# A graph layer on one core: one edge tile in 24 fetched row by row, and a reordered end

## The chip, the cores and the metric

The kernel runs on one core of a Trainium2 chip. Its time is the device time of one execution in microseconds (us). Several runs of the kernel before and after are compared, and one execution of each is profiled: every instruction of every engine with start and duration, and every DMA packet. The engines are PE (matmuls), DVE (vector), ACT (scalar), POOL (GpSimd) and SP (which only issues DMAs). SP and ACT each have a queue that issues plain DMAs in order. POOL issues indirect DMAs (gathers), whose descriptors it writes itself.

## What is computed

A relational graph convolution behind a layer norm, on 12500 nodes of 256 features and 212500 edges of 8 types; the edges are sorted by destination, and each node's last edge is its self loop:

```
h = maximum(layernorm(x), 0)
hx = einsum('ni,rio->rno', h, weight)        # 8 types
msg = hx[edge_type, src]
agg = segment_sum(msg, dst, 12500)
out = x + agg * sqrt(0.5) + bias + (h @ loop_weight) * sqrt(0.5)
```

The kernel sums the rows of h by destination and type first and multiplies by the weights afterwards, which gives the same.

## The kernel before

**Edge tiles.** Edges go in 1581 tiles of 128; two tiles are a unit (791 units, the last with one tile). For each tile the rows `h[src]` of its 128 edges come into a buffer `msg` of 128 x 256 (1 KB a row). DVE makes one-hot columns by (destination, type) (line 992, four tiles at a time), PE multiplies the rows with them (`edge_sums`, line 1030, four matmul instructions a tile), and DVE adds a unit's sums into a ring `acc` of node columns (`add_sums`, line 1063). A tile's one-hots reach over 13 of 22 destination columns (104 wide) or 17 (136 wide: `REACH`), but for the units of the last block from row `NARROWED` on, which take the whole width (176); `TAPER` sets how many units that is at the end.

**Where the rows come from.** The first tiles are gathered from x and normalised in place; in the meantime the kernel normalises x into a table h32 in HBM, and from then on tiles are gathered from that. Line 935 is the gather: one indirect DMA on POOL for a tile. `goal(t)` says how far gathers are emitted ahead of tile t: 64 tiles at first, falling to 24 at tile 370, and to 8 at the end. A ring of 66 buffers (33 pairs) holds the tiles.

**Tiles fetched row by row.** A tile with `t % SINGLE == SINGLE - 1` (SINGLE = 28), once h32 has been in use for a while and 16 tiles before the end at the latest (`single_rows`, line 907), isn't gathered. `begin_fetch` takes its buffer FAR = 36 tiles ahead, or when its gather would be emitted if that is earlier; HOLD = 8 tiles later SP and ACT each load 2 x 32 row addresses into registers (line 956) and issue 64 plain DMAs of 1 KB (line 964), four queue items on each per tile of the loop (`fetch`). PE waits by count for all 128 rows (line 1027).

**Node groups.** Nodes go in 98 groups, the first of 84 nodes and the others of 128; the ring holds six (SLOTS). When a group's last unit is added, `group_work` puts its work into `queue`: 2 products of its own rows with the loop weight and 16 with the types' weights (line 1237, two matmul instructions each), then `finish`: two additions on DVE (lines 1225 and 1252), and the store to `out`. Groups go in sets of four (XG). A set's rows of x and h come with one load each on SP (line 1180), into one of 6 row buffers in turn; the result replaces the x rows, and is stored from there. `finish` stores a whole set with one DMA of 512 KB (line 1257) at its last group, and single groups (128 KB, line 1254) for the first group and for the last set (groups 96 and 97). It then also clears or begins a ring slot, and starts loads of later sets. Every sixth group `wrap` adds the ring's overlap to its start (line 1209).

**The order of the work** is the order of emission in the loop over tiles, written out by hand: fetches and gathers, one-hots, edge sums of tile t, `finish` of groups that are due, side work, items from `queue`, and then the sums of finished units (`add_sums`), which put groups into the queue. The queue is spread: each item has a tile from which it may be issued (`ready`) and one by which it must (`until`), and a budget per tile is worked out from these. Each engine runs its instructions in this order. In the last SOON = 8 units sums are added without a lag of one unit; for the last 8 groups `ready` is the next tile and `until` at most six tiles after it.

Of the kernel before, what the change touches and what calls it, by code (L numbers as in the profile page):

```python
# [20 lines left out]
SP = mybir.EngineType.SP  # L21
ACT = mybir.EngineType.Activation

P = 128
# [4 lines left out]
XG = 4  # L29
# [13 lines left out]


WIN = 22
TAPER = 4
REACH = ((0, 13), (5, 17))

GROUP = 128
# [11 lines left out]
NEXT = 24  # L61
CLOSE = 8

SINGLE = 28
FETCH = 4
SOURCES = 32
BY_SP = (0, 2)
HOLD = 8
FAR = 36
COUNTERS = 4  # L70
LANDINGS = 68

# [3 lines left out]
PAIR = 2  # L76
# [6 lines left out]
SOON = 8  # L83
# [165 lines left out]
def kernel(  # L249
# [11 lines left out]
    nc = tc.nc  # L261
# [8 lines left out]
    plan = Plan(N, E)  # L270

    NT = plan.NT
# [41 lines left out]

    NARROWED = max(0, (row_of(NU - 1)[1] + 1 - TAPER) // PAIR * PAIR)

# [11 lines left out]
    with ExitStack() as main:  # L328
# [29 lines left out]
        msg, oh, offsets, kind = {}, {}, {}, {}  # L358
        firsts, stops, loops, marked, typed, gidx, col = {}, {}, {}, {}, {}, {}, {}
        added, zeroed = {}, {}  # L360
        single, fetches = {}, {SP: [], ACT: []}
        counters = [tc.alloc_semaphore(f"rows{i}") for i in range(COUNTERS)]
        fetched, summed = {}, {}
        landings = [tc.alloc_semaphore(f"landed{i}") for i in range(LANDINGS)]
# [389 lines left out]
        done = {"norm": 0, "weights": False, "late": [], "tile": None, "free": 0, "step": False}  # L754
# [50 lines left out]
        for d in range(0, N, XG * P):  # L805
            k = min(XG, (N - d) // P)
# [98 lines left out]
        def single_rows(t):  # L905

            return (t % SINGLE == SINGLE - 1 and t + 2 * NEAR < NT
                    and state["h32"] is not None and t // QUAD * QUAD >= state["h32"] + LATE + AHEAD)
# [67 lines left out]
        def fetch(n):  # L976
            for list_ in fetches.values():
                for _ in range(n):
                    if list_ and list_[0][0] <= done["tile"]:
                        list_.pop(0)[1]()  # L980
# [184 lines left out]
        def shorts(q):  # L1165

            return int(plan.ends[XG * q] - plan.starts[XG * q] < P)
# [46 lines left out]
        def group_work(g):  # L1214

            d0 = plan.starts[g]
            s0, n = slot(g)
            first_dep = [True]
            final = plan.NG - 1 if plan.NG > SLOTS + 1 else None

            def biased(g):
                q, k = divmod(g, XG)
                n = plan.ends[g] - plan.starts[g]
                rows_ = got["x", q]
                nc.vector.tensor_add(rows_[:n, k, :], rows_[:n, k, :], outs[g % 2][:n, 1, :])  # L1225

            def product(r, c, g=g):
                n = plan.ends[g] - plan.starts[g]
                if (r, c) == (R, 0):
                    got["out", g] = outs[g % 2][:, 0, :]  # L1230
                if r == R:
                    while ("self", g) not in got:
                        advance(None)
                    lhs, rhs = got["self", g][:, c, :n], wl[:, c, :]
                else:
                    lhs, rhs = acc[:, c, r, s0 : s0 + n], w[:, c, r * D : (r + 1) * D]
                i = nc.tensor.matmul(got["out", g][:n], lhs, rhs, start=(r == R and c == 0),  # L1237
                                     stop=(r == R - 1 and c == KC - 1))
                latest["pe"] = in_run(
                    "loops" if r == R else "products", i, r >= R - 1 and c == KC - 1).ins  # L1240
                if (r, c) == (R, 0) and g < 2:
                    tc.add_manual_dep(i.ins, done["bias"], SYNC_DEP, reason="one engine at a time")
                if r < R and first_dep[0]:
                    first_dep[0] = False
                    tc.add_manual_dep(i.ins, added[plan.last[g]].name, SYNC_DEP, reason="sums complete")

            def finish():
                q, k = divmod(g, XG)
                rows_ = got["x", q]
                if g != final:  # L1250
                    biased(g)
                nc.vector.tensor_add(rows_[:n, k, :], rows_[:n, k, :], got["out", g][:n])  # L1252
                if XG * (q + 1) >= plan.NG or n < P:
                    nc.sync.dma_start(out[d0 : d0 + n], rows_[:n, k, :])
                elif k == XG - 1:
                    first = plan.starts[XG * q + shorts(q)]
                    nc.sync.dma_start(
                        out[first : d0 + n].rearrange("(k p) d -> p k d", p=P), rows_[:, shorts(q) :, :])
                b = g + SLOTS
                q, k = divmod(b, XG)  # L1260
                if b < plan.NG:
                    if q < plan.typed:
                        clear(b)
                    else:
                        begin(b)
                if q + 1 >= plan.typed and XG * (q + 1) < plan.NG:
                    if k == XG // 4:
                        load_groups("h", h32, q + 1)
                    if k == XG - 2:
                        mark(q + 1)  # L1270
                    if k == XG - 1:
                        find_types(q + 1)

            def last():
                done["late"].append((done["tile"] + REST, finish))

            work = []
            for r in [R, *range(R)] if g != final else range(R):
                for c in range(KC):
                    work.append((0.55, lambda r=r, c=c: product(r, c)))  # L1280
            work.append((0.0, last))
            if final is not None and g == final - 1:
                work.append((0.0, lambda: biased(final)))
                for c in range(KC):
                    work.append((0.55, lambda c=c: product(R, c, final)))
            return work

        with tc.manual_schedule():
# [24 lines left out]
            for bound, lines in ((low, plan.low), (high, plan.high)):  # L1313
                whole = small.tile([P, NB], I32, name="whole")
                f = small.tile([P, NB], F32, name="bound_f")
# [98 lines left out]
                    moments_by_scalar(begun[t], [msg[i] for i in ts[-SHARED:]], len(ts) - SHARED)  # L1414

            queue = []
            waiting = []
            credit = 0.0
            late = done["late"]
# [9 lines left out]
            for t in range(NT):  # L1429
# [3 lines left out]
                while gathered < min(NT, goal(t)):  # L1433
                    gather(gathered)
                    gathered += 1
                fetch(FETCH)
                blocks_ahead(t)
                credit = min(0.0, credit) + SHARE - (0.52 if t % PAIR else 0.0)
# [35 lines left out]
                while writes and credit > 0:  # L1474
                    _, cost, f = writes.pop(0)
# [6 lines left out]
                while (background and background[0][0] <= t and not held()  # L1482
                       and (credit > 0 or background[0][0] <= t - OVERDUE)):
                    step()
                    credit -= 0.65
                budget = total = 0.0
                for _, until, c, _ in queue:
                    total += c
                    budget = max(budget, total / max(1, until - t) + 1e-9)
                while queue and (budget > 0 and t >= queue[0][0] or t >= queue[0][1]):  # L1490
                    _, _, c, f = queue.pop(0)
                    budget -= c
                    f()
                if t % PAIR == PAIR - 1 or t == NT - 1:
                    waiting.append((t // PAIR, ps))
                while waiting and (len(waiting) > LAG or t >= NT - SOON * PAIR):
                    u, ps = waiting.pop(0)
                    add_sums(u, ps)
                    while (next_group < plan.NG and plan.last[next_group] <= u
                           and (done["weights"] or (NT <= 400 and done["norm"] == len(pieces)))):  # L1500
                        g = next_group
                        while background and NT <= 400:
                            step()
                        until = PAIR * (plan.first[g + SLOTS] - 3) - REST if g + SLOTS < plan.NG else NT - 1
                        ready = t + max(0, min(DELAY, NT - 1 - t - 2 * DELAY))
                        if g >= plan.NG - SOON:
                            ready = min(ready, t + 1)
                        until = max(ready, min(until, ready + int(GROUP / plan.rate * PAIR)))
                        if g >= plan.NG - SOON:
                            until = min(until, ready + DELAY)  # L1510
                        if g and g % SLOTS == 0:
                            wrap(g)
                        work = [] if g else group_ahead(0)
                        work += group_work(g)
                        if g + 1 < plan.NG:
                            work[-8:-8] = group_ahead(g + 1)
                        for c, f in work:
                            queue.append((ready, until, c, f))
                        next_group += 1
            while background:  # L1520
                step()
            while held():
                advance(None)
            state["general"] = nc.values_load(flag[0:1, 0:1], min_val=0, max_val=1)
            while queue or late:
                if late:
                    late.pop(0)[1]()
                else:
                    queue.pop(0)[3]()


    with tc.If(state["general"]):
# [26 lines left out]
```

## Time and profile before

| | before |
|---|---|
| runs (us) | 1952.87, 1955.55, 1956.66; median 1955.55 |
| profiled execution (us) | 1955.61 |
| its span (us) | 1953.9 |
| granted TensorE clock, mean | 0.952 |
| instructions | 40535 |

The span runs from the first to the last instruction of the program; the rest of the execution's time lies outside it. A row of a group of instructions gives line, engine, operation and tiles written and read (out<-in), their number, busy time in all and mean ns of one, and behind the bar the idle time of that engine just before them and what ended it. "issue" is idle time in which the engine waited for nothing that the profile shows. PEld is PE's loading of weights; an engine with a q (SPq) is its queue of DMA issues and waits. Rows by tile give min/median/max of the duration in ns and the first and last start. Rows of waits give total, number and longest, in us. Rows by stretches of time give start:end, length, then busy us and number of instructions for PE, PEld, DVE, ACT and POOL, the granted clock, the DMA engines' busy share and GB/s. Rows in order of time give start and duration in us.

### The profile page before, as it was taken

To read this page: it belongs to the slowest core of one execution; us is meant where nothing else is said; L and a number is where in the kernel's file an instruction comes from. 1 tells how busy PE (TensorE), PEld (TensorE's weight loads), DVE (VectorE), ACT (ScalarE), POOL (GpSimd) and SP (SyncE) were. 2 spreads that over 40 slices of the span, in tenths; PEclk is the share of its full clock that TensorE was granted. 3 is DMA by queue.
4 is the path that set the end of the run, shared out by engine and by line. 5 is a ranking of instruction groups with operands and counts; after the bars stand their busy time and mean duration, and the time that the engine had idled before them with its cause. 6 is when DMAs were issued, how large, how long until landed. Compare 5 with 4: busy or idle time off the path is not lost.

```text
span 1953.9 us, 40535 instructions
## 1 busy us (share of the span) xinstructions
PE 1697.5 (87%) x10161; PEld 1457.6 (75%) x10161; DVE 1305.8 (67%) x3284; ACT 157.3 (8%) x333; POOL 1455.3 (74%) x1557
## 2 busy tenths in 40 slices
PE   1358999999999999889899988998889899898998
PEld 1347898998877777777777777777777777687887
DVE  6768766887765786656677656578466568666652
ACT  6778200000000000000000000000000000000000
POOL 7777777777777777777777777777777777777774
PEclk9559999999999999999999999999999989999999
DMA  8984454545444444444544444534444444444432
GB/s 273 353 276 128 123 153 122 152 133 141 122 143 132 130 142 120 133 131 121 151 131 122 141 131 121 150 111 142 130 121 142 130 123 131 121 142 126 130 112 82
DMA packets 158374, 279.41 MB, mean 143 GB/s; under 512 B 35392, under 2 KB 109142, under 8 KB 158134
## 3 DMA queue, kind: packets, MB, share of 16 engines
q0 software_dynamic: 73488, 200.77, 35.6%
q1 hardware_dynamic: 76600, 72.73, 12.0%
q10 hardware_dynamic: 8046, 3.30, 0.9%
q8 instruction: 80, 1.31, 0.3%
q14 instruction: 160, 1.31, 0.2%
HBM read 251.06 MB, written 25.60 MB: 142 GB/s over the span
## 4 chain that ended last, share of the span: by engine, by line
PE 38%; DMA 22%; POOL 20%; issue 9%; DVE 6%; ACT 4%; SPq 1%; DVEq 0%; POOLq 0%; ACTq 0%; PEldq 0%
POOL msg L935 20%; PE po L1237 19%; DMA msg<-h,gidx 19%; PE ps L1030 18%; DMA xt<-in_x_dram 2%; ACT msg L872 1%; DVE acc L1063 1%; ACT xt L872 1%; DVE stats L828 1%; DVE acc L1105 1%; SPq L964 1%; PE pt L1087 1%; DVE oh L992 1%; DVE moves L455 0%; ACT unused L841 0%
## 5 line engine op out<-in xcount | busy, mean ns | idle before, releaser
L935 POOL DMA_INDIRECT msg<-h,gidx x1431 | 1358.6, 949 | 438.3 <-issue 372.5
L1030 PEld LDWEIGHTS ps<-oh,msg 128*128 128x128 f32 x6324 | 928.2, 197 | 397.2 <-DMA msg<-h,gidx 251.7
L1030 PE MATMUL ps<-oh,msg 128*128 128x136 f32 (+1 forms) x6324 | 1008.5, 289 | 212.4 <-DMA msg<-h,gidx 127.0
L1237 PE MATMUL po<-w,acc 128*128 128x256 f32 (+1 forms) x3136 | 892.8, 390 | 7.6 <-DVE acc L1063 7.4
L1063 DVE TENSOR_TENSOR acc<-acc,ps 128x352 f32 x791 | 409.3, 517 | 409.1 <-PE ps L1030 399.4
L1237 PEld LDWEIGHTS po<-w,acc 128*128 128x128 f32 (+1 forms) x3136 | 520.0, 194 | 45.0 <-DVE acc L1063 10.1
L1105 DVE SCALAR_TENSOR_TENSOR acc<-types,pt 128x256 f32<-128x256 bf16 x688 | 249.1, 414 | 65.4 <-PE pt L1087 59.5
L992 DVE TENSOR_TENSOR oh<-fixed,cols 128x544 f32<-128x544 f32 x396 | 283.3, 716 | 0.0
L935 POOL DMA_INDIRECT msg<-in_x_dram,gidx x100 | 94.8, 948 | 38.9 <-issue 30.5
L1237 PE MATMUL po<-wl,self_t 128*128 128x256 f32 (+1 forms) x392 | 112.0, 410 | 7.2 <-DVE acc L1063 4.3
L1237 PEld LDWEIGHTS po<-wl,self_t 128*128 128x128 f32 (+1 forms) x392 | 71.4, 203 | 15.5 <-DVE acc L1063 5.3
L872 ACT ACTIVATE msg<-msg,shift,rstd 128x256 f32<-128x256 f32 x100 | 50.8, 586 | 6.0 <-DVE stats L836 4.6
L872 ACT ACTIVATE xt<-xt,shift,rstd 128x256 f32<-128x256 f32 x98 | 50.0, 587 | 13.1 <-DVE shift L869 12.7
L1225 DVE TENSOR_TENSOR xr<-xr,po 128x256 f32<-128x256 f32 (+1 forms) x98 | 40.6, 414 | 12.3 <-PE po L1237 5.3
L1252 DVE TENSOR_TENSOR xr<-xr,po 128x256 f32<-128x256 f32 (+1 forms) x98 | 41.2, 421 | 10.6 <-PE po L1237 7.3
L828 DVE BATCH_NORM_STATS2 stats<-xt 128x6 f32<-128x256 f32 x98 | 34.3, 411 | 17.9 <-DMA xt<-in_x_dram 17.7
L1087 PE MATMUL pt<-ident,hr 128*128 128x128 f32 (+1 forms) x196 | 38.6, 279 | 5.6 <-DMA hr<-h 3.7
L1092 DVE COPY self_t<-pt 128x256 f32<-128x256 f32 (+1 forms) x98 | 40.7, 415 | 3.1 <-PE pt L1087 2.9
L1159 DVE CAST types<-pt 128x512 bf16<-128x512 f32 x22 | 15.2, 691 | 40.6 <-PE pt L1155 40.6
L455 DVE TENSOR_SCALAR moves<-fixed 128x271 int32<-128x271 int32 (+1 forms) x90 | 40.6, 451 | 1.6 <-DVE acc L1063 0.5
L457 DVE COPY_PREDICATED fixed<-moves,fixed 128x311 int32<-128x311 int32 (+14 forms) x90 | 38.0, 422 | 3.1
L1087 PEld LDWEIGHTS pt<-ident,hr 128*128 128x128 f32 (+1 forms) x196 | 25.4, 151 | 8.1 <-DMA hr<-h 3.9
(166 smaller groups left out, 349.3 us busy)
## 6 DMA issues: line engine op xcount, KB each, us to landing
msg<-h ACTq DMA_DIRECT2D x3200, 1.0 KB
msg<-h SPq DMA_DIRECT2D x3200, 1.0 KB
msg<-h,gidx POOLq DMA_INDIRECT x1431
xt<-in_x_dram SPq DMA_DIRECT2D x24, 512.0 KB
h<-xt SPq DMA_DIRECT2D x24, 512.0 KB
xr<-in_x_dram SPq DMA_DIRECT2D x23, 512.0 KB
hr<-h SPq DMA_DIRECT2D x23, 512.0 KB
out_dram<-xr SPq DMA_DIRECT2D x23, 512.0 KB
```

The costliest lines, as they stand in the source:

```text
L455: nc.vector.tensor_single_scalar(m, packed[:, :n], 1 << (bit + k), op=ALU.bitwise_and)
L828: in_run("stats", nc.vector.bn_stats(stats[:n, k, :], row), row is here[-1])
L872: nc.scalar.activation(row, row, AF.Relu, bias=shift[:n, j : j + 1], scale=rstd[:n, j : j + 1])
L935: i = nc.gpsimd.indirect_dma_start(out=msg[t], out_offset=None, in_=table[:, :], in_offset=bass.IndirectOffsetOnAxis(ap=gidx[b][:, at : at ...
L992: j = nc.vector.tensor_tensor(o[:, k : k + v, :i, :width], iota_f[:, :width].unsqueeze(1).unsqueeze(1).to_broadcast([P, v, i, width]), of. ...
L1030: j = nc.tensor.matmul(ps[:, c, first : first + width], m[:, c * P : (c + 1) * P], o[:, :width], start=(i == 0 and c == 0), stop=(end and ...
L1063: i = nc.vector.tensor_tensor(a, a, ps, op=ALU.add)
L1087: in_run("turns", nc.tensor.transpose(pst[:, c, :n], rows_[:n, c * P : (c + 1) * P], ident[:n, :n]), c == KC - 1)
L1092: nc.vector.tensor_copy(got["self", g][:, :, :n], pst[:, :, :n])
L1105: i = nc.vector.scalar_tensor_tensor(acc[:, :, r, s0 : s0 + n], of, float(r + 1), pst[:, :, :n], op0=ALU.is_equal, op1=ALU.mult)
L1237: i = nc.tensor.matmul(got["out", g][:n], lhs, rhs, start=(r == R and c == 0), stop=(r == R - 1 and c == KC - 1))
L1252: nc.vector.tensor_add(rows_[:n, k, :], rows_[:n, k, :], got["out", g][:n])
```

## The change

One tile in 24 instead of 28 is fetched row by row, its buffer taken 44 tiles ahead instead of 36. The store of a whole set is no longer issued in `finish` but put on a list, from which the loop takes it 24 tiles later, ahead of that tile's fetches; the last two sets (groups 92 to 97) are stored group by group, at once. For the last eight groups the queue's items are ready at the tile at which the group is done, and in the last 16 tiles items are issued after the sums are added, not before. `TAPER` falls from 4 to 2, so that four more tiles are narrow.

```diff
-TAPER = 4
+TAPER = 2
...
-SINGLE = 28
+SINGLE = 24
...
-FAR = 36
+FAR = 44
+STORE = 24
...
-        single, fetches = {}, {SP: [], ACT: []}
+        single, fetches, stores = {}, {SP: [], ACT: []}, []
...
-                if XG * (q + 1) >= plan.NG or n < P:
+                if XG * (q + 2) >= plan.NG or n < P:
                     nc.sync.dma_start(out[d0 : d0 + n], rows_[:n, k, :])
                 elif k == XG - 1:
                     first = plan.starts[XG * q + shorts(q)]
-                    nc.sync.dma_start(
-                        out[first : d0 + n].rearrange("(k p) d -> p k d", p=P), rows_[:, shorts(q) :, :])
+                    to, of = out[first : d0 + n].rearrange("(k p) d -> p k d", p=P), rows_[:, shorts(q) :, :]
+                    stores.append((done["tile"] + STORE, lambda: nc.sync.dma_start(to, of)))
...
+            def issue(t):
+                budget = total = 0.0
+                for _, until, c, _ in queue:
+                    total += c
+                    budget = max(budget, total / max(1, until - t) + 1e-9)
+                while queue and (budget > 0 and t >= queue[0][0] or t >= queue[0][1]):
+                    _, _, c, f = queue.pop(0)
+                    budget -= c
+                    f()
...
+                while stores and stores[0][0] <= t:
+                    stores.pop(0)[1]()
                 fetch(FETCH)
...
-                budget = total = 0.0
-                for _, until, c, _ in queue:
-                    total += c
-                    budget = max(budget, total / max(1, until - t) + 1e-9)
-                while queue and (budget > 0 and t >= queue[0][0] or t >= queue[0][1]):
-                    _, _, c, f = queue.pop(0)
-                    budget -= c
-                    f()
+                if t < NT - SOON * PAIR:
+                    issue(t)
...
                         if g >= plan.NG - SOON:
-                            ready = min(ready, t + 1)
+                            ready = t
...
+                if t >= NT - SOON * PAIR:
+                    issue(t)
...
+            while stores:
+                stores.pop(0)[1]()
```

More of the change, by code (lines that the diff above doesn't have):

```diff
@@ L1529 @@
                     queue.pop(0)[3]()
+                while stores:
+                    stores.pop(0)[1]()
     with tc.If(state["general"]):
```

## The prediction

> **What bounds the kernel now.** I read the page first, for which engine is never free and what the others wait for.
>
> ```profile
> span 1953.9 us, 40535 instructions
> ...
> PE 1697.5 (87%) x10161; PEld 1457.6 (75%) x10161; DVE 1305.8 (67%) x3284; ACT 157.3 (8%) x333; POOL 1455.3 (74%) x1557
> ...
> L935 POOL DMA_INDIRECT msg<-h,gidx x1431 | 1358.6, 949 | 438.3 <-issue 372.5
> ...
> L1030 PE MATMUL ps<-oh,msg 128*128 128x136 f32 (+1 forms) x6324 | 1008.5, 289 | 212.4 <-DMA msg<-h,gidx 127.0
> ```
>
> By busy time PE looks like the bound (87%) and POOL free for a quarter. But POOL's idle time is "issue": it waited for nothing, it needs that time around each gather. 1358.6 busy plus 438.3 idle over 1431 gathers is 1.256 us each. The same instructions by tile, the waits, and the busy time by stretches show how steady that is.
>
> ```profile
> L964 ACTq DMA_DIRECT2D msg<-h x3200: 217/228/784, 219.2 to 1817.9; - x189
> ...
> L964 SPq DMA_DIRECT2D msg<-h x3200: 227/228/1072, 223.9 to 1876.5; - x189
> L935 POOL DMA_INDIRECT msg<-h,gidx x1431: 940/946/1246, 136.6 to 1932.2; - x179
> L935 POOL DMA_INDIRECT msg<-in_x_dram,gidx x100: 942/946/1109, 4.8 to 135.3; - x100
> ```
>
> ```profile
> POOL msg L935 <- issue: 403.1, 1308, 2.2
> ```
>
> ```profile
> 200.00:300.00 100.00, 98.42 (x646) 91.26 (x647) 69.63 (x176) 11.87 (x13) 74.40 (x79) 0.98 0.48 139
> ...
> 500.00:600.00 100.00, 92.01 (x558) 79.32 (x557) 63.43 (x145) 0.00 (x0) 75.58 (x81) 0.97 0.47 132
> ...
> 1700.00:1800.00 100.00, 91.94 (x574) 79.56 (x573) 60.71 (x134) 0.00 (x0) 75.70 (x80) 1.00 0.46 133
> ```
>
> POOL gathers from 4.8 to 1932.2 us, and each stretch of 100 us holds 79 to 81 of them, whether PE is full (200 to 300, where it works off what was gathered ahead) or waits for gathers (from about 500 on). Its longest idle stretch is 2.2 us. So nothing holds POOL back: **the number of gathers sets when the last tile arrives**, at 100/80 = 1.25 us each. PE has room: between 200 and 300 it did 646 matmuls where the steady state needs about 560.
>
> The time is then 1531 gathers (1531 x 1.25 = 1914 us), the steps after the last one, and what lies outside the span. The profiled execution took 1955.61 us (span 1953.90), the three timed runs have a median of 1955.55, so the sum made on the one holds for the other.
>
> **The change, part by part.**
>
> *Fewer gathers.* 3200 rows on each of two queues, 64 a tile, are 50 tiles fetched row by row; with 1431 + 100 gathers that is the 1581 tiles. Before, they are tiles 167, 195, ..., 1539. The 100 gathers from x mean that the table h is in use from tile 100, and the rule at line 907 admits rows 64 tiles after that; tile 143 falls before that point, tile 167 after it. So after: 167, 191, ..., 1559, which is 59 tiles. Nine gathers go: 9 x 1.25 = **-11.25 us** at the last gather. Nothing on POOL takes their place.
>
> *Rows of nine more tiles, on SP and ACT.* This is 1152 more DMAs of 1 KB, and 18 more loads of 32 addresses on each queue.
>
> ```profile
> 1108.50 33.25 SPq L964 DMA_DIRECT2D msg<-h  x86
> 1164.21 0.41 SPq L1257 DMA_DIRECT2D out_dram<-xr  x1
> 1164.67 0.50 SPq L1180 DMA_DIRECT2D hr<-h  x1
> 1169.03 23.40 SPq L964 DMA_DIRECT2D msg<-h  x64
> ```
>
> ```profile
> L956 SPq TENSOR_LOAD <-single x100: 2049/2180/3752, 221.5 to 1863.8; - x100
> ```
>
> A row takes 23.40/64 = 0.366 us of its queue, and a tile 23.4 plus some 2.7 for its address loads, 26.1 us. Per fetched tile come about 0.5 us of other issues on SP (three per 65 tiles). 24 tiles pass in 23 x 1.25 = 28.75 us (before: 28 in 33.75), so SP would be 26.6/28.75 = 93% taken, against 79%. I cost it at **nothing**: the work hides behind gathers as long as a row stays under 0.40 us. If that cover goes, PE waits for rows, and that is the rival that ends slower.
>
> *Buffers taken 44 tiles ahead* moves the start of a fetch 8 tiles (10 us) forward. Issues run from 8 to 25 tiles after it (66 items, 4 a tile), so the last row is issued 19 tiles before its use, not 11. The ring holds 66 tiles and gathers lead by 24 from tile 370 on, so no earlier reader is met. 0 us, and it pays for the fuller queue.
>
> *Stores 24 tiles later.* The store stands on SP ahead of rows, h and x loads, and waits for DVE:
>
> ```profile
> SPq L1257 <- DVE acc L1063: 213.9, 16, 24.1
> SPq L1257 <- DVE xr L1252: 187.7, 8, 55.8
> ```
>
> 401.6 us of waits in 24 places (above, between 1108.50 + 33.25 and 1164.21), in which rows stood behind the store. SP was ahead of its time there, so this costs nothing today. Afterwards the store meets a sum long done, and SP may run 24 tiles further ahead. A row buffer is kept 24 tiles longer; it is wanted again three sets of four groups (194 tiles) later. 0 us, and without it the 93% would not fit.
>
> *The end.* The tail in order of time (tiles are counted back from the last gather, tile 1580):
>
> ```profile
> 1898.46 0.95 POOL L935 DMA_INDIRECT msg<-h,gidx  x1 [0.30 <-issue]
> ...
> 1901.26 0.69 PE L1030 MATMUL ps<-oh,msg 128*128 128x104 f32 x4 [0.56 <-DMA msg<-h,gidx]
> ...
> 1918.25 0.41 SPq L1257 DMA_DIRECT2D out_dram<-xr  x1
> 1918.46 0.95 POOL L935 DMA_INDIRECT msg<-h,gidx  x1 [0.30 <-issue]
> ...
> 1920.07 0.53 PEld L1030 LDWEIGHTS ps<-oh,msg 128*128 128x128 f32 x4 [0.22 <-DMA msg<-h,gidx]
> ...
> 1924.00 1.18 PE L1030 MATMUL ps<-oh,msg 128*128 128x104 f32 x8 [3.20 <-DMA msg<-h,gidx]
> 1924.73 0.52 DVE L1063 TENSOR_TENSOR acc<-acc,ps 128x352 f32 x1 [3.83 <-PE ps L1030]
> ...
> 1925.29 0.53 DVE L1209 TENSOR_TENSOR acc<-acc 128x352 f32<-128x352 f32 x1
> ...
> 1926.45 2.57 PE L1237 MATMUL po<-w,acc 128*128 128x256 f32 x6
> ...
> 1928.86 0.59 PE L1030 MATMUL ps<-oh,msg 128*128 128x104 f32 x4
> ...
> 1929.29 1.91 PE L1237 MATMUL po<-w,acc 128*128 128x256 f32 x8
> ...
> 1931.04 0.76 PE L1030 MATMUL ps<-oh,msg 128*128 128x176 f32 x4
> ...
> 1932.22 0.95 POOL L935 DMA_INDIRECT msg<-h,gidx  x1 [0.30 <-issue]
> ...
> 1937.57 3.74 PE L1030 MATMUL ps<-oh,msg 128*128 128x176 f32 x24
> ...
> 1941.96 7.17 PE L1237 MATMUL po<-w,acc 128*128 128x256 f32 x32 [0.64 <-DVE acc L1063]
> 1949.17 0.42 DVE L1252 TENSOR_TENSOR xr<-xr,po 128x256 f32<-128x256 f32 x1 [7.27 <-PE po L1237]
> ```
>
> ```profile
> 1904.80:1908.20 3.40, 3.25 (x10) 2.80 (x11) 0.82 (x2) 0.00 (x0) 2.75 (x3) 0.50 0.39 116
> 1925.30:1928.70 3.40, 3.40 (x10) 2.69 (x9) 1.61 (x3) 0.00 (x0) 2.49 (x4) 0.50 0.32 99
> ```
>
> An undisturbed tile's sums start 2.80 us after its gather (1898.46 to 1901.26). Tile 1569's gather starts at 1918.46 and its sums only at 1924.00, 2.74 late: the 512 KB store issued at 1918.25 lies beside it. From there PE never waits for a gather: the last tile's data are due at 1932.22 + 2.80 = 1935.0, and PE, with group 96's products in between, begins its sums near 1940.7 (the sixth of six tiles in 1937.57 + 3.74). So the tail hangs on 1924.00.
>
> - The store becomes four of 128 KB, each when its group is done, the last near tile 1563. Ends: 0, and -2.74 for no collision. A quarter of the bytes delays by 0.7 at most, and PE arrives there with little to spare (0.22 us idle before tile 1568, at 1920.07), so I take **-2.4**.
> - After the stall the granted clock is 0.50 for 3.4 us (second window): six products' matmuls take 2.57, 0.43 each, where eight take 1.91 later, 0.24 each. 3.4 us at half pace are 1.7 lost. Without a stall of 3 us I expect full pace: **-1.7**; ends 0 and -1.7, as the first window shows half clock behind waits of only 0.5 us each.
> - Four tiles (1572 to 1575) are narrow: at most 0.76 - 0.59 = 0.17 each, less for the two of 136 columns, **-0.6** in all, DVE's share hidden.
> - Products at once: group 96 starts behind tile 1569's sums instead of 1570's, and its first product with summed columns waits for the add and the wrap on DVE (0.52 + 0.53, plus 0.2 to be seen) with four matmuls of its own rows (4 x 0.24) as cover and no further tile's. Behind that wait stand tile 1570's sums and all else on PE. I take **+0.5**; ends 0 and +0.8.
>
> The Trainium skill's page "TensorE: Matmul & The Clock Gate" ("What's actually happening") says that the clock falls to half after an idle window of about 3.4 us, watched in a free-running window. By that rule a tail with waits under 1 us loses nothing and the term is the full -1.7. The first window speaks against taking it as certain, so both ends stay in the range.
>
> Sum: -11.25 - 2.4 - 1.7 - 0.6 + 0.5 = -15.45, from 1955.61: **1940.2 us**. The floor holds: the last gather's data would be due at 1935.0 - 11.25 = 1923.8 and PE takes them at 1940.7 - 15.45 = 1925.2, so the tail stays PE's by 1.4 us, and gathers and tail together can't give more than 11.25 + 5.7 = 17 (1938.6).
>
> **Rivals.**
>
> *The nine gathers alone count (0.25).* The tail keeps half clock or a stall elsewhere: 1955.6 - 11.25 is 1944.4, with some of the terms 1943 to 1946. For it: half clock occurs twice in the last 50 us. Against it: the one big stall has a visible cause that goes.
>
> *The row queues become the bound and it is slower (0.05).* Place: SP, lines 956 and 964. It decides when SP needs more per fetched tile than before's pace for 24 tiles, 24 x 33.75/28 = 28.9 us, that is at (28.9 - 3.2)/64 = 0.40 us a row. At 0.42 a tile costs 30.1, 1.2 over; from tile 450 on, 47 fetched tiles lose 56 us, less the lead of 19 tiles (23 us): 33 us, so 1988. For it: 93% of a queue in order, and waits for DVE on the four single stores and the last index block. Against it: 86 rows in 33.25 (0.39, a wait for addresses among them) and 64 in 23.40 while both queues run. The Trainium skill's page "DMA: Bandwidth & Descriptors" ("Rules for kernel authors") says to coalesce small transfers, since under 64 KB one pays mostly overhead; that is this rival's rule, as the rows are 1 KB. The trace agrees that overhead is what is paid, 0.366 us for 1 KB, but on queues that the end doesn't wait for.
>
> *The change doesn't do what it says (0.03).* If a tile isn't begun in time, POOL gathers it after all and only the tail is left: -4.2, 1951.4. Against it: the request is made at a lead of 44 or, while gathers lead by more, at the gather itself.
>
> **How the numbers follow.** The forecast (1937 to 1943) has 0.60, the nine alone 0.25, rows that come late now and then (1946 to 1951) 0.04, no fewer gathers 0.03, slower 0.05, and under 1937 0.03. The range leaves out the slow cases and takes in the runs' own spread (1952.87 to 1956.66): 1936.5 to 1946.0. A measurement of this kernel tells about 0.2% (3.9 us) from no change. Faster than 1951.6: 0.92; within 0.2%: 0.03; slower: 0.05.
>
> **What would show it.** POOL: 1522 gathers, still 79 to 81 in 100 us, the last starting near 1921. SP: 3776 rows, hardly a wait at line 1257, 26 us per tile. PE: no wait of 3 us near tile 1569 and no half clock behind it; sums of tile 1580 near 1925. Wrong would be idle time of PE behind line 1027's waits, gathers under 78 in 100 us, or a gap of POOL ended by PE.

## The result, and the profile after

The changed kernel takes 1978.74 us (median of 4 runs, 1977.32 to 1981.31) against 1955.14 before: a ratio of 1.0124 with a 95% interval of 1.0112 to 1.0136. It is 1.2% slower, where 1940.2 us was forecast. The profiled execution took 1978.5 us with a span of 1976.8. One line was added above the code in question, so what was line 935 is 936, 964 is 965, 1027 is 1028 and 1030 is 1031.

The page of the changed kernel, as far as it answers to the lines shown of before:

```profile
span 1976.8 us, 42924 instructions
...
PE 1665.7 (84%) x10161; PEld 1510.1 (76%) x10161; DVE 1301.7 (66%) x3284; ACT 157.3 (8%) x333; POOL 1448.0 (73%) x1548
...
SPq 32%; PE 30%; DMA 16%; issue 9%; DVE 6%; ACTq 5%; ACT 3%; PEldq 0%; POOL 0%; DVEq 0%
...
L936 POOL DMA_INDIRECT msg<-h,gidx x1422 | 1351.0, 950 | 471.9 <-issue 371.6
...
L1031 PE MATMUL ps<-oh,msg 128*128 128x136 f32 (+1 forms) x6324 | 989.8, 289 | 263.2 <-PEq L1028 185.4
```

The nine gathers are gone (1422 + 100), each costs what it did (950 ns), and the whole takes longer. The third line, the chain that ended last, has changed hands: SP's queue holds 32% of it, and POOL nothing. PE's idle time ahead of its sums is no longer ended by gathers but by line 1028, where it waits for rows that were fetched singly. Before, that wait of PE and POOL's wait for PE's sums were these rows:

```profile
PE ps L1030 <- PEq L1027: 3.5, 2, 2.2
```

```profile
POOL msg L935 <- PE ps L1030: 53.7, 168, 1.8
```

In the changed kernel PE waits 185.4 us there (above), and POOL's row is:

```profile
POOL msg L936 <- PE ps L1031: 84.6, 180, 3.4
```

POOL now stands for PE: gathers may be emitted only 24 tiles ahead of the sums, and a PE that waits for rows lets POOL run into that limit. The stretches of 100 us show it as missing gathers (the number in the POOL column). Three of them:

```profile
600.00:700.00 100.00, 80.11 (x492) 73.30 (x492) 58.17 (x137) 0.00 (x0) 74.08 (x79) 0.88 0.49 139
...
800.00:900.00 100.00, 85.14 (x507) 76.59 (x508) 56.08 (x124) 0.00 (x0) 71.21 (x75) 0.88 0.45 125
...
1000.00:1100.00 100.00, 79.53 (x472) 72.57 (x471) 72.13 (x189) 0.00 (x0) 72.27 (x77) 0.86 0.45 125
```

Between 400 and 1800 us a stretch holds 75 to 81 gathers, where before it held 80 or 81. The granted clock is 0.86 to 0.88 in these three, where it was 0.93 to 1.00 in the same stretches before: PE now stands still for up to 10.7 us at a time. By tile:

```profile
L965 SPq DMA_DIRECT2D msg<-h x3776: 227/228/4356, 216.4 to 1926.0; - x199
...
L965 ACTq DMA_DIRECT2D msg<-h x3776: 217/228/562, 218.0 to 1902.4; - x199
L936 POOL DMA_INDIRECT msg<-h,gidx x1422: 940/947/1283, 135.7 to 1957.3; - x178
```

The last gather starts at 1957.3. The forecast put it at 1932.2 - 11.25 = 1921: **36 us of the 38.5 between forecast and result were lost ahead of that gather**, the rest in the tail.

SP's queue fetched rows from 216.4 to 1926.0: 1709.6 us for 59 tiles, 29.0 us a tile (9 us of the whole are a wait at an index block), where 24 tiles last 28.75. Before, 1652.6 us for 50 tiles held 305 us of waits at stores (the 401.6 less one of 55.8 us ahead of the first row and one of 41.0 behind the last), which leaves 27.0 a tile. A stretch of SP in the changed kernel, in order of time, shows that only loads of addresses and other issues are left between the rows:

```profile
689.94 42.18 SPq L965 DMA_DIRECT2D msg<-h  x101
732.17 0.41 SPq L1181 DMA_DIRECT2D hr<-h  x1
734.87 24.36 SPq L965 DMA_DIRECT2D msg<-h  x64
759.33 0.42 SPq L1259 DMA_DIRECT2D out_dram<-xr  x1
759.87 0.48 SPq L1181 DMA_DIRECT2D xr<-in_x_dram  x1
763.94 26.16 SPq L965 DMA_DIRECT2D msg<-h  x60
```

64 rows take 24.36 us where they took 23.40, and 60 take 26.16 (each stretch with a load of addresses among the rows). The store at 759.33 is issued without any wait, as the change meant. The chain of the changed kernel has a second thing in it, the time between the issue of a row and its landing (four of 17 such pieces among the longest of the chain):

```profile
731.89 11.48 DMA msg<-h
...
853.61 14.21 DMA msg<-h
...
1290.69 16.02 DMA msg<-h
...
1783.54 15.55 DMA msg<-h
```

10 to 16 us from issue to landing, for 1 KB. The first of these belongs to the stretch above: SP had issued the tile's last row by 732, and PE began its sums at 743.4.

### The profile page after: what moved, and what is told of

Read it like the earlier page. It is cut to its first block, busy times and chain, and to the rows that moved or that the text cites. A ratio compares the mean times of both kernels' runs of the same rounds, so it can differ in the third digit from the quotient of the medians.

```text
span 1976.8 us, 42924 instructions
## 1 busy us (share of the span) xinstructions
PE 1665.7 (84%) x10161; PEld 1510.1 (76%) x10161; DVE 1301.7 (66%) x3284; ACT 157.3 (8%) x333; POOL 1448.0 (73%) x1548
## 2 busy tenths in 40 slices
DMA packets 160312, 279.57 MB, mean 141 GB/s; under 512 B 36448, under 2 KB 111350, under 8 KB 160054
## 4 chain that ended last, share of the span: by engine, by line
SPq 32%; PE 30%; DMA 16%; issue 9%; DVE 6%; ACTq 5%; ACT 3%; PEldq 0%; POOL 0%; DVEq 0%
SPq L965 26%; PE po L1238 15%; PE ps L1031 13%; DMA msg<-h 11%; SPq L957 5%; ACTq L965 4%; DMA xt<-in_x_dram 2%; DMA msg<-h,gidx 1%; DVE acc L1064 1%; ACT xt L873 1%; ACT msg L873 1%; ACTq L957 1%; DVE stats L829 1%; DMA w<-in_L_gnn_weight_dram 1%; DMA spans<-in_dst_dram 1%
## 5 line engine op out<-in xcount | busy, mean ns | idle before, releaser
L1031 PEld LDWEIGHTS ps<-oh,msg 128*128 128x128 f32 x6324 | 971.8, 203 | 360.6 <-PEq L1028 199.7
L1031 PE MATMUL ps<-oh,msg 128*128 128x136 f32 (+1 forms) x6324 | 989.8, 289 | 263.2 <-PEq L1028 185.4
L1238 PE MATMUL po<-w,acc 128*128 128x256 f32 (+1 forms) x3136 | 902.7, 393 | 11.7 <-DVE acc L1064 11.3
L1238 PEld LDWEIGHTS po<-w,acc 128*128 128x128 f32 (+1 forms) x3136 | 525.5, 196 | 51.0 <-DVE acc L1064 15.0
L1238 PE MATMUL po<-wl,self_t 128*128 128x256 f32 (+1 forms) x392 | 117.3, 426 | 6.3 <-DVE acc L1064 4.3
L1226 DVE TENSOR_TENSOR xr<-xr,po 128x256 f32<-128x256 f32 (+1 forms) x98 | 40.5, 413 | 23.7 <-PE po L1238 17.5
```

Source lines behind the costliest of these rows:

```text
L1031: j = nc.tensor.matmul(ps[:, c, first : first + width], m[:, c * P : (c + 1) * P], o[:, :width], start=(i == 0 and c == 0), stop=(end and ...
```

## The experiments

Two theories at first. **A:** the rows of nine more tiles put the two queues over what 24 tiles last. **B:** the later stores do the harm, since SP and ACT now issue rows at the same time. Within A: is it SP's own sum of issues (A2), a place behind both queues where rows hold each other up (A1), or just the time that a row takes to land?

**One in 28 with all the rest of the change.**

```diff
-SINGLE = 24
+SINGLE = 28
```

> The changed kernel with one tile in 28 fetched row by row again (50 tiles, 1531 gathers); all else of the change stays: 44 tiles ahead, stores 24 tiles later, the new end. Theory A (nine more tiles put SP's queue over what 24 tiles last): PE's waits at line 1028 fall from 185 us to under 20, POOL runs through, and only the end gains: 1950 to 1953. Theory B (the later stores do the harm, since SP and ACT now issue rows at the same time where a waiting SP used to leave ACT alone): rows still come late, and it stays over 1960.

It took 1951.28 us beside 1953.48 for the kernel before on the same chip, a ratio of 0.9988 (0.9978 to 0.9997). PE waits for gathers again and not at line 1028:

```profile
POOL msg L936 <- issue: 405.3, 1311, 2.0
...
PE ps L1031 <- DMA msg<-h,gidx: 137.1, 228, 3.6
```

So theory B falls: with later stores, buffers 44 tiles ahead and the new end, 50 tiles cost nothing. The loss comes with the step from 28 to 24. This run also shows the new end alone, below.

**One in 24 alone, in the kernel before.**

```diff
-SINGLE = 28
+SINGLE = 24
```

> The kernel before with one change: one tile in 24 is fetched row by row. Buffers are taken 36 tiles ahead, stores stand where they stood, the end is as before. Theory A: SP now has 29 us of rows and loads in 28.75 us and on top of that waits for DVE at 24 stores (400 us before): slower than the whole change, 1985 to 2010. Theory B: without the later stores it is better than the whole change, 1940 to 1965.

1990.6 us in a single run, 12 us more than the whole change, as A expected. Its waits, of PE and of SP:

```profile
PE ps L1030 <- PEq L1027: 198.3, 43, 16.4
```

```profile
SPq L1257 <- DVE xr L1252: 99.3, 7, 56.2
...
SPq L1257 <- DVE acc L1063: 20.9, 11, 6.4
```

SP's waits at stores have shrunk from 401.6 to 120 us on their own, and 81 of these lie ahead of the first row or behind the last: a queue that is full is no longer ahead of its time. The later stores could save only the 39 us that are left.

**SP's rows alone.** ACT's half of a fetched tile comes with two plain DMAs of 32 rows each, so as many bytes arrive, but from wrong rows (this half of the fetched tiles is left out of the computation). ACT's loads of addresses go with its single rows.

```diff
-                    lambda r=r, engine=engine: load_sources(t, r, engine)))
+                    (lambda r=r: block_of_rows(t, r)) if engine == ACT
+                    else (lambda r=r, engine=engine: load_sources(t, r, engine))))
...
+            j = nc.scalar.dma_start(msg[t][r0 : r0 + SOURCES, :], h32[r0 : r0 + SOURCES, :])
```

> The changed kernel, in which ACT no longer fetches its 64 rows of a tile singly but 2 blocks of 32 consecutive rows of h with one plain DMA each (wrong rows: this part of the gather is left out); SP's half is as it was, 64 single rows and 2 loads of addresses a tile. Theory A1 (rows of both queues meet in one place behind the queues and hold each other up): SP's issues shorten from a mean of 0.27 to about 0.23 us, a tile costs SP 26 to 27 us instead of 29, rows land sooner, PE's waits at line 1028 nearly vanish: 1938 to 1945. Theory A2 (SP's own issue time is too long, whatever ACT does): SP still needs 29 us a tile and PE's waits stay over 100 us: 1965 to 1980.

1940.11 us in a single run, the time that was forecast for the change. SP issues the same 3776 rows:

```profile
L966 SPq DMA_DIRECT2D msg<-h x3776: 227/228/857, 215.2 to 1879.0; - x199
L937 POOL DMA_INDIRECT msg<-h,gidx x1422: 942/946/1284, 136.5 to 1919.0; - x178
L981 ACTq DMA_DIRECT2D msg<-h x118: 317/432/1425, 215.2 to 1791.3; - x118
```

1663.8 us for 59 tiles are 28.2 a tile, and some 90 us of the whole are now waits (at stores and at index blocks), so some 27 of work a tile. PE's wait at the fetched tiles falls from 185.4 us to 21.8 (line 1040 here), and the pieces of the chain between issue and landing shrink:

```profile
PE ps L1043 <- PEq L1040: 21.8, 10, 5.2
```

```profile
421.68 1.58 DMA msg<-h
475.14 1.91 DMA msg<-h
554.55 1.72 DMA msg<-h
661.45 2.27 DMA msg<-h
```

**In these chains a row lands 1.6 to 2.3 us after its issue when SP alone fetches singly, and 10 to 16 us after it when ACT does so too.** SP's instructions are the same in both runs, so A2 by itself falls: what makes SP's sum too long, and the rows late, is ACT's 3776 single rows (or their address loads, which went with them). That they meet somewhere behind the queues is shown; where (one of the DMA engines, or what writes their descriptors) is not.

A chain holds only the rows that held something up. The traces also tell for every fetched tile but the last four how long its last row took, from the later of the two queues' last issues to the last update of the tile's row counter. The median is 12.0 us in the changed kernel, 9.8 at one in 26 (the next run), 5.7 at one in 28, 5.1 in the kernel before and 1.7 with SP alone. So rows are late whenever both queues fetch singly, and the later the more rows the two issue in the same time. The changed kernel holds the same comparison within itself. ACT once waits for an index block and issues no row for 43 us:

```profile
1549.84 4.00 ACTq L965 DMA_DIRECT2D msg<-h  x12
1596.08 1.19 ACTq L419 DMA_DIRECT2D spans<-in_dst_dram  x3
1597.37 2.58 ACTq L965 DMA_DIRECT2D msg<-h  x8
```

The tile that SP fetches in that time, its last row issued at 1582.81, lands 2.6 us after that. The time passes before the transfer starts: ACT's 3776 rows are 3776 packets of 1024 bytes on a queue of their own, and, paired in order, a packet starts 8.0 us (median) after its row's issue and takes 0.08 us (mean).

**One in 26 with the rest of the change.**

```diff
-SINGLE = 24
+SINGLE = 26
```

> The changed kernel with one tile in 26 fetched row by row (54 tiles, 1527 gathers). 26 tiles last 25 x 1.25 = 31.25 us against SP's 29.2 us a tile. Theory A: SP keeps up, four gathers (5 us) and the gain of the end count: 1944 to 1949. If rows that land late are the trouble whatever the rate, PE's waits at line 1028 stay over 100 us and it takes over 1960.

1947.01 us, ratio 0.9965 (0.9951 to 0.9979): faster than both kernels, as expected.

```profile
PE ps L1031 <- DMA msg<-h,gidx: 126.2, 202, 2.2
...
POOL msg L936 <- PE ps L1031: 51.1, 164, 1.1
```

PE hardly waits at line 1028 (2.5 us, once), and POOL runs through. Four gathers are 5.0 us, and 6.5 were gained. Rows land almost as late as in the changed kernel (9.8 us against 12.0), so late landing alone doesn't cost the time; what costs it is a queue that needs longer for a fetched tile than the time from one such tile to the next.

**Which place, and whether an earlier begin helps.** The other runs fell on three other chips (0, 6 and 3; the four runs above fell on chip 14), on which the kernel before takes 2412 to 2445 us, 23 to 25% longer. They are read only against the kernel before on the same chip. They can't answer the two questions for the first chip, since the queues' own instructions take longer there: a MOVE between two of SP's rows, 29 ns at most in the traces of the kernels before and after, takes up to 1448 ns in the run with one in 26 alone, and SP needs 38 us and more for a fetched tile. With rows issued so slowly the queues don't hold each other up: both fetch singly, and still a tile's last row lands 0.9 to 1.6 us after its issue (medians of these runs, taken as above). SP's queue holds 43 to 54% of the chain that ended last in these runs; what bounds the kernel there is SP's own sum.

Rows named as 4 or 16 parts, meant to spread a row over several DMA engines:

```diff
-                    msg[t][r0 + i : r0 + i + 1, :].bitcast(U8), h32_bytes[:, bass.ds(v, D * 4)])
+                    msg[t][r0 + i : r0 + i + 1, :].bitcast(U8).rearrange("p (a b) -> p a b", a=4),
+                    h32_bytes[:, bass.ds(v, D * 4)].rearrange("p (a b) -> p a b", a=4))
```

> The changed kernel; each row's DMA names its 1024 bytes as 4 parts of 256, on both sides, so that a row may go as four packets side by side. Number of DMAs, bytes and issuers are the same. If the place where rows meet is one DMA engine that moves the single packets one after another, the parts spread, rows land sooner and SP's issues shorten: 1938 to 1950. If the place is ahead of the engines and its work goes by DMA or by packet, nothing is gained, and with four times the packets it gets slower: 1977 to 2100.

> As the run with 4 parts, but 16 parts of 64 bytes. One engine as the place: 1938 to 1950. A place whose work goes by packet: far slower than with 4 parts, over 2000. A place whose work goes by DMA: 1970 to 1985, as the changed kernel.

2547.6 and 2542.36 us against 2412.01 (1.056 and 1.054). The pages of the changed kernel and of the one with 4 parts have the same packets, and so has the one with 16, which shows that the parts were joined again and that the edit did nothing:

```profile
DMA packets 160312, 279.57 MB, mean 141 GB/s; under 512 B 36448, under 2 KB 111350, under 8 KB 160054
```

```profile
DMA packets 160312, 279.57 MB, mean 110 GB/s; under 512 B 36448, under 2 KB 111350, under 8 KB 160054
```

They say nothing on the place, but they stand for the changed kernel on that chip: 1.055, with 326 and 294 us of PE's waits for fetched rows.

Loads of x and h for later sets issued by ACT:

```diff
-                nc.sync.dma_start(
+                (nc.scalar if q > 3 else nc.sync).dma_start(
```

> The changed kernel (one in 24) with the loads of x and h for the later sets issued by ACT instead of SP. SP is rid of some 0.4 us a fetched tile, ACT gets it. If SP's own sum (29.0 against 28.75 us) decides, this brings it under: PE's waits at line 1028 fall by more than half, 1945 to 1962. If the place where both queues' rows meet is full, nothing changes: 1970 to 1985.

Three more runs of the same kernel:

> The same kernel as e8 (one in 24, loads of x and h on ACT), once more on a chip where the kernel before takes its usual time. SP's own sum decides: PE's waits at line 1028 fall by more than half, 1945 to 1962. The place behind the queues is full: 1970 to 1985.

> One tile in 24, loads of x and h on ACT (as e8 and e9, which ran on a chip where the kernel before took 25% longer). SP's own sum decides: PE's waits at line 1028 fall from 185 us by more than half, 1945 to 1962. The place behind the queues is full: 1970 to 1985.

> One tile in 24, loads of x and h on ACT. SP's own sum decides: PE's waits at line 1028 fall from 185 us by more than half, 1945 to 1962. The place behind the queues is full: 1970 to 1985.

2540.06, and in the repeats 2586.7, 2571.72 and 2573.6 us: 1.053 to 1.058 of before, with 309 to 334 us of PE's waits at line 1028. Nothing gained, but that doesn't settle it: SP still needs 38.0 us for a fetched tile in the first of these runs, and 24 tiles last some 35.5 us on that chip (an estimate: 28.75 x 2412.01/1953.48), so it was over by more than these loads weigh.

Buffers 56 tiles ahead:

```diff
-FAR = 44
+FAR = 56
```

> The changed kernel (one in 24) with the buffers taken 56 tiles ahead instead of 44, so that a fetch may begin 12 tiles (14 us) earlier. If rows come late because they take long to land, this hides it: under 1955. If the queues are full from the first fetch to the last, an earlier begin has nothing to draw on: 1970 to 1982.

Three more runs of it:

> The changed kernel with buffers taken 56 tiles ahead (as e11). Landing time is the trouble: under 1955. The queues are full from the first fetch on: 1970 to 1982.

> The changed kernel with buffers taken 56 tiles ahead. Landing time is the trouble: under 1955. The queues are full from the first fetch on: 1970 to 1982.

> The changed kernel with buffers taken 56 tiles ahead. Landing time is the trouble: under 1955. The queues are full from the first fetch on: 1970 to 1982.

2582.43, and in the repeats 2593.26, 2581.52 and 2543.22 us: 1.053 to 1.062, with 260 to 306 us of waits there. Nothing gained either, which fits a queue that is busy from its first row to its last. Landing took 1.4 to 1.5 us here, so whether an earlier begin would help where it takes 12 stays open.

One in 25, and one in 26 alone in the kernel before:

> The changed kernel with one tile in 25 fetched row by row. 25 tiles last 24 x 1.25 = 30.0 us, SP took 29.0 us a tile in the changed kernel and 28 at one in 26. By the theory that only a queue over its time counts, it still fits: two or three gathers fewer than one in 26 has, 1942 to 1947. If queues near their limit are already late, PE's waits at line 1028 come back: 1950 to 1970.

> The kernel before with one tile in 26 fetched row by row, nothing else changed (36 tiles ahead, stores where they stood, the end as before). Beside the run of the whole change at one in 26 (1947.0) it prices the later stores and the earlier buffers below the queue's limit. If they matter (SP stands at stores with rows behind them, and has only 2 us a tile to spare): rows late, over 1955. If SP's waits at stores only use up spare time: four gathers fewer, 1948 to 1951.

and two more runs of the latter:

> The kernel before with one tile in 26 alone (as e10). Later stores and earlier buffers matter below the limit: over 1955, against 1947.0 with the whole change at one in 26. SP's waits at stores only use up spare time: 1948 to 1951.

> The kernel before with one tile in 26 alone. Later stores and earlier buffers matter below the limit: over 1955, against 1947.0 with the whole change at one in 26. SP's waits at stores only use up spare time: 1948 to 1951.

One in 25 took 2495.77 us, 1.034 (1.0265 to 1.0415) of before. (With an odd step a fetched tile can be the first of its unit, which the order of this kernel isn't made for; sums of such units are not computed rightly there, since the table of row addresses holds only the second tile of a unit, so the time is that of a like amount of work.) One in 26 alone took 2497.29, 2490.07 and 2497.3 us, 1.022, 1.0211 and 1.022 of before, with intervals of about half a per cent to each side. A fetched tile takes SP 38.9 us at one in 25 and 40.2 in the first run at one in 26, where 25 and 26 tiles last some 37 and 39 us (estimates, as above), so both are over its limit; they don't price the later stores below it, and that stays open.

## Why the prediction was wrong

**The step that failed is "Rows of nine more tiles, on SP and ACT. I cost it at nothing".** In its place SP needed 29.0 us for a fetched tile instead of 26.6, where 24 tiles last 28.75, and PE waited 185.4 us for rows. The place and the sign are those of the second rival, which had a chance of 0.05 and its turning point at 0.40 us a row. By the same reckoning (a tile's issues and loads, less 3.2) the changed kernel's 29.0 us make (29.0 - 3.2)/64 = 0.403 us a row: just past the point. The rival's size was wrong too: by its own sum 0.1 us over, 47 times, less a lead of 23 us, would have cost nothing. Three things in that step were wrong.

- *The row price was taken at a lighter load.* For the kernel before it is nearly right: 27.0 us a tile without the waits at stores, 26.6 forecast. (The 23.40 us of 64 rows hold one of the tile's two loads of addresses, so a row by itself takes 0.33 us and not 0.366; the tile's sum is the same.) But the instruction that issues a row takes SP 0.266 us in the changed kernel, where it took 0.235 before (means over all rows in the traces), and 64 times the difference are the 2 us between 27.0 and 29.0. The run with ACT's singles replaced, 0.233 us, shows that it is the other queue that makes the difference.
- *A row was counted as there when it was issued.* "Issued 19 tiles before its use" are 23 us; 12.0 of them (median) went in landing. One piece of this could have been seen before: the chain of the kernel before has one row piece of 8.59 us, at 499.54. By itself this did not cost, as the run with one in 26 shows.
- *93% taken was called cover.* That sum goes by the gathers' pace, which holds only once PE waits for gathers. Ahead of that PE works off the tiles gathered ahead: in the changed kernel it passes tiles 143 to 287 in 144.1 us, 24.0 us for 24 tiles, while a fetched tile takes SP over 28. So the cover is used up at the start. By the traces the last row of tile 167 lands 31.5 us before PE's first sum of that tile, and the last row of tile 287 only 0.1 us before; from there to tile 1463 it is 0.1 us for 43 of the 50 fetched tiles, so the rows set PE's pace. At 29.0 us against 28.75 nothing wins the cover back. With one in 26 it is used up as well (0.1 us at tile 311), but 31.25 us a fetched tile let it grow again, to 55.5 us at tile 1169. The kernel before came near it too: PE's two waits for fetched rows there, 3.5 us in all, lie at 508 and 570 us.

**Fewer gathers, -11.25 us:** right in itself. With the row queues unburdened the last of 1522 gathers starts at 1919.0 (forecast 1921), and the whole takes 1940.11 us (forecast 1940.2). That the two times agree to 0.1 us is luck: the last gather is 2 us earlier than forecast, and the tail behind it is 2 us longer (1938.4 - 1919.0 = 19.4 us, where 21.7 - 4.2 = 17.5 was forecast). In the changed kernel POOL is held by the sums instead, 31 us more than before.

**Buffers taken 44 tiles ahead, 0 us, "and it pays for the fuller queue":** the 0 fits the run with one in 28; the second half was wrong. A queue that is never idle can't begin earlier.

**Stores 24 tiles later, 0 us:** right at one in 28. The waits at stores were slack of a queue ahead of its time, as said (though rows stood behind only 305 of the 401.6 us); at one in 24 they shrank to 120 us by themselves.

**The end, -4.2 us:** right in kind where it can be seen alone. In the run with one in 28 the tail in order of time is:

```profile
1924.92 0.69 PE L1031 MATMUL ps<-oh,msg 128*128 128x104 f32 x4 [0.54 <-DMA msg<-h,gidx]
1925.44 1.05 PE L1238 MATMUL po<-wl,self_t 128*128 128x256 f32 x4
1926.78 1.13 PE L1238 MATMUL po<-w,acc 128*128 128x256 f32 x4 [0.29 <-DVE acc L1210]
...
1936.94 3.59 PE L1031 MATMUL ps<-oh,msg 128*128 128x104 f32 x24
```

```profile
1924.00:1941.20 17.20, 15.73 (x93) 13.88 (x91) 6.88 (x15) 0.00 (x0) 9.60 (x11) 1.00 0.33 97
```

Tile 1569 waits 0.54 us instead of 3.20, the wrap costs a wait of 0.29 (forecast +0.5), and the clock is 1.00 to the end of the sums. From the last gather's start to the end of the span it is 1953.5 - 1935.7 = 17.8 us, where it was 1953.9 - 1932.2 = 21.7: -3.9. That is one profiled execution of each; by the medians of the runs the whole gained 2.2 us (1953.48 to 1951.28), about half of the forecast. In the changed kernel the tail is 1976.8 - 1957.3 = 19.5 us, as tile 1569 waits longer again:

```profile
1948.03 0.69 PE L1031 MATMUL ps<-oh,msg 128*128 128x104 f32 x4 [1.91 <-DMA msg<-h,gidx]
```

A store of 128 KB lies beside that tile's gather, but so does one in the run with one in 28, so the cause of this wait stays open. The term for half clock hangs on chance, as both ends in the forecast said: the wait of 1.91 us above has full clock behind it. With one in 26 it came again, behind waits of 0.51 and 1.63 us:

```profile
1913.42 0.73 PE L1031 MATMUL ps<-oh,msg 128*128 128x136 f32 x4 [0.51 <-DMA msg<-h,gidx]
1915.79 0.69 PE L1031 MATMUL ps<-oh,msg 128*128 128x104 f32 x4 [1.63 <-DMA msg<-h,gidx]
```

```profile
1916.50:1919.90 3.40, 3.40 (x10) 2.60 (x10) 2.14 (x4) 0.00 (x0) 2.59 (x3) 0.50 0.36 99
```

The rule that I had weighed, from the Trainium skill's page "TensorE: Matmul & The Clock Gate" ("What's actually happening"), asks for an idle window of some 3.4 us. Here the clock fell to half behind 2.1 us of waiting in all, so the trace does not agree with the rule as I read it, and the trace decides.

**A rule that the prediction left out.** The Trainium skill's page "DMA: Bandwidth & Descriptors" says under "Issuing engines are not separate DMA queues" that DMAs of all issuers end on the same 16 engines and interleave, and that several issuers save only issue time. The prediction weighed another rule of that page and left this one out; the run with SP's rows alone agrees with it (a tile's last row lands 1.7 us after its issue with one issuer of single rows, 12.0 with two, medians).

## What to carry to other kernels

Work moved off a bound engine to a queue that looks idle has to be priced at the load that it will have then: add up the queue's whole time per period, with its neighbours' load in the same stretch included, and set it against its reader's pace in every stretch. Where the reader is faster than its steady pace the lead is used up, and only room in the steady pace wins it back: in this case 28 us of 31.25 (waits taken out, one in 26) did, and 29.0 of 28.75 didn't. Waits of a queue that runs ahead of its time are not a reserve to be freed; they vanish by themselves as it fills. Where a change overshoots a limit, a smaller step of the same change may be the gain: one tile in 26 with the rest of the change gave 0.35%, one in 24 lost 1.2%. The limit is not the same on every chip: on the three slower ones, one in 26 alone lost 2%.

## What the runs showed of the hardware

- With both SP and ACT issuing single-row DMAs of 1 KB, the last row of a tile lands 5.1 us after its issue at 3.9 rows per us (kernel before, medians), 9.8 us at 4.2 (one in 26) and 12.0 us at 4.4 (changed kernel), while the DMA engines are busy some 45% of the time on the mean; with SP alone it is 1.7 us. The instruction that issues a row grows only from 0.233 to 0.266 us. ACT's half of the bytes as two DMAs of 32 rows a tile does no such harm. On the slower chips, at 3.2 to 3.4 rows per us, both queues' rows land in 0.9 to 1.6 us.
- Half clock on PE for 3.4 us behind waits of 0.51 and 1.63 us with matmuls between them (one in 26), and full clock behind a wait of 1.91 us (changed kernel).
- Naming a contiguous row of 1 KB as 4 or 16 parts changes no packet (160312 in all three runs).
